# The first feed-forward's first product in seven block products, with two engines' orders written by hand

## The chip, the cores and the metric

The kernel runs on one core of a Trainium2 chip. The metric is the device time of one execution in microseconds, as the median of several runs. In the text PE is TensorE (matmul), PEld its weight loads, DVE is VectorE, ACT is ScalarE, POOL is GpSimd, and SP is the engine that only issues DMAs here. A letter q behind an engine's name means its instruction queue.

## The reference, cut to what matters

64 graphs of 256 nodes and 256 features go through two layers. The first is a graph attention layer with a feed-forward block of 1024 hidden features, the second a transformer layer with attention that is masked by relation, and a feed-forward block of its own. All is float32.

```python
# layer 0, per graph
h = gat(x, adj, W1, a1); h = gat(h, adj, W2, a2)      # softmax over neighbours, twice
h = layernorm(x + h, g_ln1, b_ln1)
ff = relu(h @ w_ff1 + b_ff1) @ w_ff2 + b_ff2          # h: 256x256, w_ff1: 256x1024
x = layernorm(h + ff, g_ln2, b_ln2)
# layer 1, per graph, 8 heads of 32
attn = softmax(q @ k.T / sqrt(32)); out = sum_r (attn * (adj == r)) @ v_r
x = layernorm(x + out @ Wo + bo, g1, beta1)
out = layernorm(x + gelu(x @ W1 + b1) @ W2 + b2, g2, beta2)
```

The change concerns the product h @ w_ff1 of layer 0, which is called the first feed-forward's first product.

## The kernel before, in words

Two graphs form a group of 512 tokens, so there are 32 groups. After a prologue the function `turn` is called 32 times. Each turn works on three groups at once, at different depths: group y is in layer 1 (attention, norm, second feed-forward), group x = y+1 is in the feed-forward of layer 0, and group z = y+2 is in the two graph attentions. An older group, y-1, still waits for its last norm, its affine step and its store (`waiting`, `finish`).

Attention of a group is cut into four quads (two graphs, four heads each). `scores(n)` makes the score products of quad n (L993), its four exponentials on ACT (L999), the masked copies ea (DVE, L1001) and the sums over node blocks es (DVE, L1004). `sums(n)` makes the weighted sums po and the totals zo on PE (L1014, L1017), and after every second quad `divided` the shares (DVE, L1025 to L1030). PE needs ACT and DVE to be done with a quad before its sums. To fill that time, eight blocks of the first feed-forward's first product (`hidden`, L804 on PE, relu on ACT at L806) stand between the quads in three groups: two, three and three blocks.

The second feed-forward's first product is already made from seven products of half the size each way (`hidden_seven`, L838). Its weights are combined once, on POOL (`seven`). For each turn DVE makes four differences of the moving operand (tt, L821). Each of the seven products comes twice, for halves a and b of the hidden features, and each half holds two PSUM banks, `one` and `two`. ACT copies a bank out to h1 (`copied`, L847), DVE adds a bank to h1 (`added`, L850), and ACT applies the function at the end (`done`, L856, and L880 for a whole row). A bank is written again by the next of the seven products only when it has been read out, so PE waits for ACT or DVE there.

After attention, `out_` multiplies by wo (yop, L766), with `project(z)` (xpp, L712) and `first_rows(z)` (L721) between. `normed` makes a norm: statistics on DVE (L780, L781), the inverse root on POOL (L782, L783), nm on DVE (L784), four applications on ACT (L787). `normed_features` transposes the normed rows (yt, DVE L666) and moves the pieces to their places by DMAs (L685 on SP's and ACT's queues, L675 on SP's) and four copies on POOL (L683, L675). PE meanwhile makes the first feed-forward's second product (yfp, L897, 64 instructions). Then come the second feed-forward's seven products, with the graph attention's sums (hpp, L755) between, then its second product, also of seven (`hidden_out_seven`, L918 on PE; four differences eq and eaq on DVE at L910 to L913; each partial result added to y by DVE at L923), and the graph attention of group z (L733 to L745, ygp at L766).

What sets the order: PE and SP run in the order of the code (`tc.manual_schedule`). The orders of DVE, ACT and POOL are made by the framework's scheduler; `behind(...)` only keeps an instruction from being put before a marked one. The stretch between the quads had, at L1137 and following,

```python
        scores(0)
        v = values(y_, hT, range(T))
        scores(1)
        piece()
        sums(0)
        first_hidden(range(0, 2))
        scores(2)
        sums(1)
        first_hidden(range(2, 5))
        scores(3)
        piece()
        first_hidden(range(5, 8))
```

and after it `early(z)` (the transposes of x and of the adjacency of group z on DVE, L1041 and L658), `load_x`, `finish` of the older group, `load_rows`, `sums(2)`, `sums(3)`. `checked` (DVE, L704) tests that the adjacency holds only 0 and 1.

Of the kernel before, what the change touches and what calls it, by code (L numbers as in the profile page):

```python
# [16 lines left out]
P = 128  # L17
# [368 lines left out]
def narrow_path(  # L386
# [213 lines left out]

    w1s, w2s = [], []

    def folding():

        shifted(wf1, range(FB // 2), lb1, bf1, "bf1")
        yield
        shifted(wf1, range(FB // 2, FB), lb1, bf1, "bf1")
        scaled(wf1, lg1)
        yield
        for w, bias, name in ((wq, bq, "bq"), (wk, bk, "bk")):  # L610
            shifted(w, range(KB), lb2, bias, name)
            scaled(w, lg2)
        yield
        ps = bank("rbvp")
        for k in range(KB):
            nc.tensor.matmul(ps, lb2[:, k:k + 1].to_broadcast([P, P]), wv[:, k].rearrange("p r f -> p (r f)"),
                             start=(k == 0), stop=(k == KB - 1))
        nc.vector.tensor_tensor(rbv, rbv, ps, ALU.add)
        scaled(wv.rearrange("p c r f -> p c (r f)"), lg2)
        shifted(w1, range(FB // 2), lb3, b1, "b1")  # L620
        yield
        shifted(w1, range(FB // 2, FB), lb3, b1, "b1")
        scaled(w1, lg3)
        w1s.extend(seven(w1, "w1"))
        w2s.extend(seven_out(w2, "w2"))
        yield
# [79 lines left out]

    def projected(u, hT):
        xp = work.tile([P, T, WX], F32, tag="wh", name=f"xp{u}")
        for t in range(T):
            ps = bank(f"xpp{u}_{t}")  # L710
# [13 lines left out]

    def gat_softmax(u, l, wh, rows, c, w, aT):

# [15 lines left out]
        nc.vector.reciprocal(z, z)  # L742
        nc.gpsimd.tensor_add(lowg, lowg, z)
        for t in range(T):
            mark["scaled"] = nc.scalar.activation(wh[:, t, :w], wh[:, t, :w], AF.Copy, scale=z[:, t:t + 1])  # L745
        return s

# [23 lines left out]
    def normed(u, l, y, blocks=range(T)):  # L771

        n, t0 = f"{u}_{l}_{blocks[0]}", blocks[0]
        bt = slice(t0, t0 + len(blocks))
# [4 lines left out]
        for t in blocks:  # L779
            nc.vector.bn_stats(st[:, t, :], y[:, t, :])  # L780
            nc.vector.bn_aggr(mv[:, t, :], st[:, t, :])  # L781
        nc.gpsimd.tensor_scalar(rs[:, bt], mv[:, bt, 1], EPS, 0.0, op0=ALU.add, op1=ALU.add)  # L782
        nc.gpsimd.tensor_tensor(rs[:, bt], rs[:, bt], mhalf[:, bt], ALU.pow)  # L783
        nc.vector.scalar_tensor_tensor(nm[:, bt], mv[:, bt, 0], -1.0, rs[:, bt],  # L784
                                       op0=ALU.mult, op1=ALU.mult)
        for t in blocks:
            mark["normed"] = nc.scalar.activation(y[:, t, :], y[:, t, :], AF.Identity,  # L787
                                                  bias=nm[:, t:t + 1], scale=rs[:, t:t + 1])
        if l == 3:
            nc.gpsimd.tensor_add(high[:, bt], high[:, bt], mv[:, bt, 0])  # L790

# [4 lines left out]

    def hidden(u, l, hT, wi, bi, func, blocks, h1=None):

        if h1 is None:
            h1 = work.tile([P, FB, TN], F32, tag="h1", name=f"h1{u}_{l}", bufs=1)  # L800
        for f in blocks:
            ps = bank(f"h1p{u}_{l}_{f}")
            for k in range(KB):
                nc.tensor.matmul(ps, wi[:, k, f * P:(f + 1) * P], hT[k],  # L804
                                 start=(k == 0), stop=(k == KB - 1))
            nc.scalar.activation(h1[:, f, :], ps, func, bias=bi[:, f:f + 1])  # L806
        return h1

    def hidden_seven(u, l, hT, w, bi, func, h1):

        a11, a12, a22, s1, s2, s3, s4 = w
        tt = work.tile([P, HPB, NB * N], F32, tag="e", name=f"tt{u}_{l}").rearrange("p a n -> p (a n)")
        quarter = [[hT[k][:, b * NB:(b + 1) * NB] for b in range(G)] for k in range(KB)]
# [42 lines left out]

        for h in halves:
            two[h] = bank(f"h1b{u}_{l}_{h}")  # L860
            product(two[h], h, a12, quarter[1][0], True)
            copied(h, 0, 0, two[h])
            one[h] = bank(f"h1a{u}_{l}_{h}")
            product(one[h], h, a11, quarter[0][0], True)
            added(h, 0, 0)
        yield
        for h in halves:
            product(two[h], h, s1, moving(0), True)
            copied(h, 1, 1, two[h])
        mark["fifth"] = mark["copied"]  # L870
        for h in halves:
            product(two[h], h, s4, quarter[1][1], False)
            copied(h, 0, 1, two[h])
        yield
        for h in halves:
            product(one[h], h, s2, moving(1), False)
            added(h, 0, 1)
            for i in range(2):
                f = 2 * h + i
                nc.scalar.activation(h1[:, f, :], h1[:, f, :], func, bias=bi[:, f:f + 1])  # L880
        yield
        for h in halves:
            product(one[h], h, s3, moving(2), False)
            added(h, 1, 1)
            done(h, 1, 1)
        yield
        for h in halves:
            product(one[h], h, a22, moving(3), False)
            done(h, 1, 0, one[h])

# [93 lines left out]
    def weighted(u, b, m, q, k_, aT):  # L984
# [13 lines left out]
        for a in range(HPB):  # L998
            mark[f"exp{b * KB + m}"] = nc.scalar.activation(e[:, a, :], ps[a], AF.Exp, scale=isd)  # L999
        for a in range(0, HPB, 2):  # L1000
            nc.vector.tensor_tensor(ea[:, a:a + 2, :], e[:, a:a + 2, :],  # L1001
                                    ab[:, None, :].to_broadcast([P, 2, NB * N]), ALU.mult)
        es = work.tile([P, HPB, N], F32, tag="es", name=f"es{n}")
        mark[f"summed{b * KB + m}"] = nc.vector.tensor_add(es, e[:, :, 0:N], e[:, :, N:2 * N])  # L1004
# [32 lines left out]
    def early(z):  # L1037
# [4 lines left out]
        d["xT"] = [xT[:, k] for k in range(KB)]  # L1042
        d["aT"] = adjacency(z, d["aq"])

    def project(z):
        d = g[z]
        d["xp"] = projected(z, d["xT"])

# [3 lines left out]
    def first_softmax(z):  # L1052
        d = g[z]
        d["s"] = gat_softmax(z, 0, d["xp"], d["rows"], F + 3, WH, d["aT"])

    def first_scores(z):
        first_rows(z)
        first_softmax(z)

    def second_rows(z):  # L1060
        g[z]["rows"] = score_rows(z, 1, g[z]["hp"], F)

    def second_softmax(z):
        d = g[z]
        d["s"] = gat_softmax(z, 1, d["hp"], d["rows"], F + 1, F, d["aT"])

# [18 lines left out]
    def out_pieces(u, y, h1, last):  # L1085
# [9 lines left out]
        for n, _ in enumerate(hidden_out_seven(u, 1, y, h1, w2s, *s)):  # L1095
            if last and n in (4, 6):
                finish(u, y, n // 6, 1)
            yield

    def finish(u, y, b, n, first=(), then=()):  # L1100

        bt = slice(b * NB, (b + n) * NB)
        with behind(*first):
            normed(u, 3, y, range(b * NB, (b + n) * NB))
        with behind(*then):
            affine(y[:, bt, :], rg4, rb4)
        nc.sync.dma_start(out[G * u + b:G * u + b + n].rearrange("b (c p) f -> p (b c) f", p=P), y[:, bt, :])

# [4 lines left out]
    def turn(y_, x_, z):  # L1113
# [8 lines left out]
        def scores(n):  # L1122
            e[n] = weighted(y_, *quads[n], q, k_, Y["aT"])

        def sums(n):
            b, m = quads[n]
            if m == 0:
                acc[b] = [psum.tile([P, 512], F32, tag=t_, name=f"{t_}{y_}_{b}") for t_ in ("po", "zo")]
            applied(b, m, v, *e.pop(n), *acc[b])
            if m == KB - 1:  # L1130
                divided(y_, b, *acc[b], oT)

        def first_hidden(blocks):
            if X:
                X["h1"] = hidden(x_, 0, X["hT"], wf1, bf1, AF.Relu, blocks, X.get("h1"))
            else:
                piece()  # L1137

        scores(0)
        v = values(y_, hT, range(T))  # L1140
        scores(1)
        piece()
        sums(0)
        first_hidden(range(0, 2))
        scores(2)
        sums(1)
        first_hidden(range(2, 5))
        scores(3)
        piece()
        first_hidden(range(5, 8))  # L1150
        if Z:
            early(z)
        if z + 1 < NG:
            load_x(z + 1)
        if waiting:
            finish(*waiting.pop(), 0, G, ("summed1", "exp2"), ("divided0",))
        if z + 1 < NG:
            load_rows(z + 1)
        sums(2)
        sums(3)  # L1160

        y = Y["y"]

        def out_(b):
            add_blocks(y_, "yop", y, b, lambda t, k: oT[:, k, t * P:(t + 1) * P],
                       lambda b, k: wo[:, k, :], KB)
        out_(0)
        piece()
        if Z:
            project(z)  # L1170
        out_(1)
        if Z:
            first_rows(z)
        normed(y_, 2, y)
        if X:
# [13 lines left out]
        h1 = work.tile([P, FB, TN], F32, tag="h1", name=f"h1{y_}_1", bufs=1)  # L1189
        for n, _ in enumerate(hidden_seven(y_, 1, hT, w1s, b1, AF.Gelu, h1)):  # L1190
            if Z and n > 1:
                Z["hp"] = gat_first(z, Z["s"], Z["xp"], Z.get("hp"), range(2 * n - 4, 2 * n - 2))
        if X:
# [6 lines left out]
        if z + 1 < NG:  # L1200
            load_adjacency(z + 1)
        if Z:
            second_rows(z)
# [21 lines left out]
    with tc.manual_schedule(engines={mybir.EngineType.PE, mybir.EngineType.SP}):  # L1225
# [19 lines left out]
        load_adjacency(2)  # L1245
        h1 = hidden(0, 0, g[0]["hT"], wf1, bf1, AF.Relu, range(FB))
        hidden_out(0, 0, g[0]["y"], h1, wf2)
        normed(0, 1, g[0]["y"])
# [60 lines left out]
```

## Time and profile before

| | us |
|---|---|
| median of 3 runs | 3142.31 (3139.66 to 3147.47) |
| the profiled execution | 3152.31 |
| its span, first to last instruction | 3150.7 |
| PE busy in the span | 3100.9 |
| DVE busy | 2234.9 |
| ACT busy | 1513.4 |
| POOL busy | 532.2 |
| PE busy in L804 (992 instructions on hT, 32 on h1T) | 450.6 and 16.3 |
| PE busy in L838 (1792 instructions) | 439.5 |

The page of a profile has one line for each group of equal instructions: line, engine, operation, what it writes and reads, shape and count; then busy time and the mean duration in ns of one; then the idle time of the engine just before them, and what ended most of it. The timeline has for each row the start and the duration in us, engine, line, operation, and in brackets the idle time of the engine before it with the instruction that ended it. An arrow `<-` in a name stands between what is written and what is read. The ends of matmuls are modelled, so rows overlap by some 0.16 us. The granted TensorE clock was 0.990 on average over the span, and 1.00 in the turn that is read.

### The profile page before, as it was taken

Reading aid. Unit: us, or ns where it says so; the run is one execution under the profiler, and the core shown is the slowest. Engines: PE = TensorE matmul, PEld = TensorE weight load, DVE = VectorE, ACT = ScalarE, POOL = GpSimd, SP = SyncE. Lnnn points to the kernel's source line nnn. Section 1 sums busy time; section 2 is a strip of 40 time slices with the busy share of each in tenths; the row PEclk is TensorE's granted clock in tenths of the full one; section 3 lists DMA queues with packets and bytes.
Section 4 is the critical chain, followed back from the end, with each engine's and each line's share of the span. In section 5 each row is a group of like instructions: output and inputs, shape, how many; then the busy total and the mean of one; then the engine's idle time right before and its main releaser. Section 6 shows DMA issues by size and latency. Waiting matters only on the chain. (4 is left out here: it accounts for less than half of the span.)

```text
span 3150.7 us, 50482 instructions
## 1 busy us (share of the span) xinstructions
PE 3100.9 (98%) x19120; PEld 2200.3 (70%) x19120; DVE 2234.9 (71%) x4280; ACT 1513.4 (48%) x2954; POOL 532.2 (17%) x822
## 2 busy tenths in 40 slices
PE   7999999999999999999999999999999999999997
PEld 5577766677766777666777666777666777667766
DVE  3577777776777777777777777777777777777665
ACT  4355544545544544545545445545445455445442
POOL 2121111111111111111211211211111211111100
PEclk8999999999999999999999999999999999999998
DMA  4011111111111111111111111111111111111000
GB/s 146 19 30 33 41 31 38 42 29 32 39 35 38 36 31 36 36 38 38 29 36 38 33 41 38 29 33 41 31 39 42 29 31 39 34 38 29 16 13 15
DMA packets 428537, 113.39 MB, mean 36 GB/s; under 512 B 364760, under 2 KB 427648, under 8 KB 428288
## 3 DMA queue, kind: packets, MB, share of 16 engines
q1 hardware_dynamic: 417952, 102.66, 14.9%
q10 hardware_dynamic: 9280, 6.39, 0.8%
q8 instruction: 153, 2.51, 0.3%
q0 software_dynamic: 1056, 1.05, 0.1%
q14 instruction: 96, 0.79, 0.1%
HBM read 57.04 MB, written 16.78 MB: 23 GB/s over the span
## 5 line engine op out<-in xcount | busy, mean ns | idle before, releaser
L804 PE MATMUL h1p<-hT,wf 128*128 128x512 f32 x992 | 450.6, 602 | 0.0
L897 PE MATMUL yfp<-wf,h 128*128 128x256 f32 x2048 | 447.3, 379 | 0.0
L897 PEld LDWEIGHTS yfp<-wf,h 128*128 128x128 f32 x2048 | 386.8, 190 | 51.8 <-issue 0.5
L787 ACT ACTIVATE y<-y,nm,rs 128x256 f32<-128x256 f32 x512 | 273.1, 598 | 249.7 <-DVE nm L784 245.4
L999 ACT ACTIVATE e<-sp 128x512 f32<-128x512 f32 x512 | 264.4, 602 | 249.3 <-PE sp L993 238.1
L1001 DVE TENSOR_TENSOR ea<-e,aT 128x1024 f32<-128x1024 f32 x256 | 312.4, 1261 | 70.9 <-ACT e L999 67.1
L804 PEld LDWEIGHTS h1p<-hT,wf 128*128 128x128 f32 x992 | 180.8, 190 | 228.6 <-issue 190.7
L806 ACT ACTIVATE h<-h1p,cols 128x512 f32<-128x512 f32 x256 | 176.9, 691 | 243.2 <-PE h1p L804 243.2
L683 POOL COPY hT<-yt 32x256 f32<-32x256 f32 x248 | 240.7, 971 | 185.1 <-DVE yt L666 177.3
L666 DVE STREAM_TRANSPOSE yt<-y 128x256 f32<-128x256 f32 x368 | 162.5, 442 | 97.4 <-ACT y L787 88.8
L782 POOL TENSOR_SCALAR rs<-mv 128x4 f32<-128x4 f32 (+1 forms) x130 | 54.6, 420 | 1043.5 <-DVE mv L781 1027.0
L977 PE MATMUL vp<-wv,hT 128*128 128x512 f32 x480 | 214.0, 599 | 0.0
L780 DVE BATCH_NORM_STATS2 st<-y 128x6 f32<-128x256 f32 x512 | 195.4, 414 | 5.6
L850 DVE TENSOR_TENSOR h<-h1a,h 128x512 f32<-128x512 f32 x192 | 131.0, 682 | 64.2 <-PE h1a L838 59.8
L966 ACT ACTIVATE q<-qp,cols 128x512 f32<-128x512 f32 x64 | 43.5, 679 | 262.5 <-PE qp L964 262.5
L993 PEld LDWEIGHTS sp<-q,k 32*128 32x128 f32 x2048 | 93.2, 184 | 108.1 <-issue 72.8
L714 ACT COPY xp<-xpp 128x260 f32<-128x260 f32 x128 | 48.1, 376 | 247.0 <-PE xpp L712 247.0
L977 PEld LDWEIGHTS vp<-wv,hT 128*128 128x128 f32 x480 | 88.7, 190 | 110.4 <-issue 103.2
L795 DVE TENSOR_TENSOR y<-y,rb 128x1024 f32<-128x1024 f32 (+1 forms) x130 | 161.7, 1245 | 3.3
L794 DVE TENSOR_TENSOR y<-y,rg 128x1024 f32<-128x1024 f32 (+1 forms) x130 | 157.3, 1210 | 5.0 <-ACT y L787 2.3
L1004 DVE TENSOR_TENSOR es<-e 128x1024 f32<-128x1024 f32 x128 | 155.8, 1217 | 0.0
L923 DVE TENSOR_TENSOR y<-yf,y 128x256 f32<-128x256 f32 x224 | 93.4, 417 | 87.7 <-PE yf L918 87.6
(217 smaller groups left out, 5686.0 us busy)
## 6 DMA issues: line engine op xcount, KB each, us to landing
hT<-yt SPq DMA_DIRECT2D x918, 32.0 KB, 2.0
y<-in_x_dram SPq DMA_DIRECT2D x32, 512.0 KB, 5.0
xq<-in_x_dram SPq DMA_DIRECT2D x240, 64.0 KB, 2.2
aq<-in_adj_dram SPq DMA_DIRECT2D x240, 64.0 KB, 2.4
out_dram<-y SPq DMA_DIRECT2D x30, 512.0 KB, 2.9
hT<-yt ACTq DMA_DIRECT2D x186, 32.0 KB, 1.9
wf<-in_L_gnn_w_ff_dram SPq DMA_DIRECT2D x2, 1024.0 KB, 7.3
w<-in_L_gnn_W_dram SPq DMA_DIRECT2D x2, 1024.0 KB
```

The source lines that it names most:

```text
L666: mark["transposed"] = nc.vector.transpose(yt[:, :, :, t].rearrange("p q k r -> p k q r"), xn[:, t].rearrange("p (k q c) -> p k q c", k=KB ...
L683: nc.gpsimd.tensor_copy(to, at)
L780: nc.vector.bn_stats(st[:, t, :], y[:, t, :])
L787: mark["normed"] = nc.scalar.activation(y[:, t, :], y[:, t, :], AF.Identity, bias=nm[:, t:t + 1], scale=rs[:, t:t + 1])
L794: nc.vector.tensor_mul(y, y, g_[:, None, :].to_broadcast(list(y.shape)))
L795: nc.vector.tensor_add(y, y, b_[:, None, :].to_broadcast(list(y.shape)))
L804: nc.tensor.matmul(ps, wi[:, k, f * P:(f + 1) * P], hT[k], start=(k == 0), stop=(k == KB - 1))
L806: nc.scalar.activation(h1[:, f, :], ps, func, bias=bi[:, f:f + 1])
L897: nc.tensor.matmul(ps[:, i * F:(i + 1) * F], h1[:, k, t * P:(t + 1) * P], wo_[:, k, :], start=(k == 0), stop=(k == FB - 1))
L977: nc.tensor.matmul(ps, hT[k][:, t * P:(t + 1) * P], wvf[:, k, :], start=(k == 0), stop=(k == KB - 1))
L999: mark[f"exp{b * KB + m}"] = nc.scalar.activation(e[:, a, :], ps[a], AF.Exp, scale=isd)
L1001: nc.vector.tensor_tensor(ea[:, a:a + 2, :], e[:, a:a + 2, :], ab[:, None, :].to_broadcast([P, 2, NB * N]), ALU.mult)
```

## The change

The eight blocks of the first feed-forward's first product are replaced by the seven products, with weights `wf1s` that POOL combines in the prologue. `hidden` is gone; `hidden_seven` no longer yields in a fixed order, but gives back a function that runs named steps: 2, 1, 5, 3, 6, 7 and 4 are the products with their copy or addition, r and s apply the function to rows that are done, and a or b names the half. The differences use the buffer of yt.

Inside the stretch from the first quad's masks to `early_adjacency`, DVE and ACT too run in the order of the code. `weighted` is cut into exponentials, `masked` and `node_sums`, `divided` is called apart (`shares`), and `normed` is cut into `norm` (statistics and POOL) and `applied_norm` (nm and the four applications). The older group's `norm`, `applied_norm` and `stored` (affine and store) stand at three places; the store and `load_rows` come behind `load_adjacency`. `load_x` comes ahead of `early`, `early` keeps only the transpose of x, and the adjacency's transpose (`early_adjacency`) comes behind the norm of group y. `project(z)` is cut into two halves. The scaling of xp (`first_scaled`) is put behind the copies of the fifth product of the second feed-forward.

```diff
@@ folding (prologue)
         scaled(wf1, lg1)
+        wf1s.extend(seven(wf1, "wf1"))
@@ turn, between the quads
-        scores(0)
-        v = values(y_, hT, range(T))
-        scores(1)
-        piece()
-        sums(0)
-        first_hidden(range(0, 2))
-        scores(2)
-        sums(1)
-        first_hidden(range(2, 5))
-        scores(3)
-        piece()
-        first_hidden(range(5, 8))
-        if Z:
-            early(z)
-        if z + 1 < NG:
-            load_x(z + 1)
-        if waiting:
-            finish(*waiting.pop(), 0, G, ("summed1", "exp2"), ("divided0",))
-        if z + 1 < NG:
-            load_rows(z + 1)
-        sums(2)
-        sums(3)
+        scores(0)
+        if z + 1 < NG:
+            load_x(z + 1)
+        with tc.manual_schedule(engines={getattr(mybir.EngineType, n) for n in
+                                         ("PE", "SP", "DVE", "Activation")[:4 if X else 2]}):
+            masks(0)
+            totals(0)
+            v = values(y_, hT, range(T))
+            steps = first_hidden(x_) if X else None
+            scores(1)
+            if Z:
+                early(z)
+            masks(1)
+            totals(1)
+            piece()
+            sums(0)
+            first("2a 1a 5a", 1)
+            scores(2)
+            sums(1)
+            shares(0)
+            first("3a 6a", 1)
+            masks(2, (0,))
+            first("2b 1b")
+            masks(2, (2,))
+            first("5b 7a 3b ra 6b")
+            totals(2)
+            first("4a 7b")
+            scores(3)
+            first("sa rb sb", 2)
+            masks(3)
+            totals(3)
+            sums(2)
+            last = norm(waiting[0][0], 3, waiting[0][1]) if waiting else None
+            if Z:
+                project(z, range(0, T // 2))
+            first("4b")
+            sums(3)
+            shares(1)
+            out_(0)
+            piece()
+            if Z:
+                project(z, range(T // 2, T))
+            out_(1)
+            if Z:
+                first_rows(z)
+            if waiting:
+                applied_norm(waiting[0][1], *last)
+            normed(y_, 2, y)
+            if Z:
+                early_adjacency(z)
@@ turn, second feed-forward
+        second("2a 1a 2b 1b 5a 5b")
+        if Z:
+            with behind("copied"):
+                first_scaled(z)
+        second("3a 3b 6a ra 6b rb")
...
         if z + 1 < NG:
             load_adjacency(z + 1)
+        if waiting:
+            with behind("added"):
+                stored(*waiting.pop(), slice(0, T))
+        if z + 1 < NG:
+            load_rows(z + 1)
@@ after the prologue's first norm
-        h1 = hidden(0, 0, g[0]["hT"], wf1, bf1, AF.Relu, range(FB))
-        hidden_out(0, 0, g[0]["y"], h1, wf2)
+        first_hidden(0)("2a 1a 2b 1b 5a 5b 3a 3b 6a ra 6b rb 7a sa 7b sb 4a 4b")
+        hidden_out(0, 0, g[0]["y"], g[0]["h1"], wf2)
```

The new function that names the steps, cut to its products:

```python
        def step(name):
            n, h = name[0], "ab".index(name[1])
            if n == "2":
                two[h] = bank(f"h1b{u}_{l}_{h}")
                product(two[h], h, a12, quarter[1][0], True)
                copied(h, 0, 0, two[h])
            elif n == "1":
                one[h] = bank(f"h1a{u}_{l}_{h}")
                product(one[h], h, a11, quarter[0][0], True)
                added(h, 0, 0)
            elif n == "5":
                product(two[h], h, s1, moving(0), True)
                copied(h, 1, 1, two[h])
            elif n == "3":
                product(two[h], h, s4, quarter[1][1], False)
                copied(h, 0, 1, two[h])
            elif n == "6":
                product(one[h], h, s2, moving(1), False)
                added(h, 0, 1)
            elif n == "7":
                product(one[h], h, s3, moving(2), False)
                added(h, 1, 1)
...
```

In the second feed-forward the order of the products is the same as before; only its steps are called by name. PE's lines shift: L838 becomes L837, L804 is gone, L923 becomes L928.

## The prediction, made before the changed kernel was run

> **What bounds the kernel now.** I read the page, then the waits of TensorE (PE), then the timeline of one turn, engine by engine. The page:
>
> ```profile
> span 3150.7 us, 50482 instructions
> PE 3100.9 (98%) x19120; PEld 2200.3 (70%) x19120; DVE 2234.9 (71%) x4280; ACT 1513.4 (48%) x2954; POOL 532.2 (17%) x822
> ...
> L804 PE MATMUL h1p<-hT,wf 128*128 128x512 f32 x992 | 450.6, 602 | 0.0
> ```
>
> PE is busy 98% of the span, and no idle time stands before L804, the product that is changed. Busy alone proves little, so I looked at who makes PE wait and at the spacing of its starts:
>
> ```profile
> PE sp L993 <- ACT k L966: 5.1, 30, 0.2
> ```
>
> This is the only wait of PE that recurs every turn: 0.2 us. The turn that starts at 1543.14 us (PE's timeline; start, us, engine, line):
>
> ```profile
> 1543.14 3.60 PE L964 MATMUL qp<-hT,wq 128*128 128x512 f32 x8
> 1546.58 3.60 PE L964 MATMUL kp<-hT,wk 128*128 128x512 f32 x8
> ...
> 1590.42 1.89 PE L766 MATMUL yop<-wo,q 128*128 128x256 f32 x8
> 1592.14 0.60 PE L721 MATMUL rows<-ident,xp 128*128 128x128 f32 x4
> ...
> 1606.40 1.03 PE L838 MATMUL h1b<-hT,w 128*128 128x256 f32 x4
> 1607.26 1.03 PE L838 MATMUL h1a<-hT,w 128*128 128x256 f32 x4
> ...
> 1609.85 1.89 PE L838 MATMUL h1b<-tt,w1s 128*128 128x256 f32 x8
> 1611.58 1.97 PE L838 MATMUL h1b<-hT,w1s 128*128 128x256 f32 x8
> 1613.38 1.89 PE L838 MATMUL h1a<-tt,w1s 128*128 128x256 f32 x8
> ...
> 1638.44 3.60 PE L964 MATMUL qp<-hT,wq 128*128 128x512 f32 x8
> ```
>
> A turn takes 1638.44 - 1543.14 = 95.30 us. From start to start a 512-column instruction takes 3.44/8 = 0.429 us, and a 256-column one (1606.40 to 1609.85, 16 of them) 0.216; each f32 product is two instructions. The seven-product form already runs there without gaps, except at 1611.58: 1.80 us for eight, 0.08 over 8 x 0.216. There PE waited for ScalarE (ACT) to copy a bank out. So PE is the bound, and what the change does to it counts nearly one for one, if nothing else becomes late.
>
> **What the Trainium skill says.** "Perfetto Trace Analysis", Identifying the Most-Contended Engine: matmul busy share is no good measure; hence the spacing. "TensorE: Matmul & The Clock Gate", Back-to-back issue gap: N/2.4 + 2.5 ns; the trace has 216 and 429 ns, which is this formula at twice the columns (215.8, 429.2). Same page, Architectural detail: PE pulls weight loads ahead, ACT and VectorE (DVE) are strict FIFOs. The 0.08 us agrees with the first; the second is why their order decides below. "ScalarE: Activation LUTs", Table sets: relu is in every set, so relu from another place loads no table; the trace agrees (loads at L880 and L737, none at L806).
>
> **The change, part by part.** t counts us from a turn's start. Orders are those of the built program, durations those of this turn.
>
> *1. Fewer columns.* 32 x 0.4294 = 13.74 us become 56 x 0.2158 = 12.09: -1.65. The row-tiled and column-tiled attention products pay about 0.1 at each change to or from the full array. The order scores(3), sums(2), xpp, 4b, sums(3) has nine changes where eight were: +0.14.
>
> *2. Handovers inside the seven products.* A product's end to ACT's start is 0.20, the copy 0.58, its end to PE's next effective start 0.16: 0.94, and one product between covers 0.864. So 0.08 of wait, as at 1611.58. It stands so at 5a (1a covers), 5b (1b) and 3b (7a): 0.24. Before 7b the sum on DVE lies between (0.20 + 0.69 + 0.16 = 1.05, covered by 4a): 0.19. The other steps have two or more products between. Sum +0.43; floor 0, ceiling 1.0 if DVE's queue is behind. I walked it: the four differences (1.7 us) follow the last v at t 16.05, the masks of quad 1 end at 21.1 and its sums at 22.3, needed at 22.7 and 24.4. ACT gains six copies and eight short activations for eight long ones, some 3 us in a stretch where it is half idle: nothing. First half of the turn: -1.65 + 0.14 + 0.43 = -1.08, so yop_1 ends at t 47.92 (before 49.00).
>
> *3. The way from yop_1 to the second feed-forward's input.* Before:
>
> ```profile
> 1595.58 0.16 DVE L784 SCALAR_TENSOR_TENSOR nm<-mv,rs 128x4 f32<-128x4 f32 x1 [1.54 <-POOL rs L783]
> 1596.41 1.92 DVE L666 STREAM_TRANSPOSE yt<-y 128x256 f32<-128x256 f32 x4 [0.67 <-ACT y L787]
> 1598.48 3.91 SPq L685 DMA_DIRECT2D hT<-yt  x6
> ```
>
> yt is done at t 55.19; the last move is issued at t 58.7, lands 1.9 later (60.6), and PE reads it at 63.26: 2.7 us of slack. After: add at 48.12; then nm of the delayed norm, and all four statistics alternate with their aggregates (0.53 a pair instead of two pairs ahead): 51.05. GpSimd and nm_2 as before (1.7): 52.75. ACT's four norms of the older output stand ahead, but end at 51.0. Then DVE runs the adjacency transpose (1.24) ahead of yt, and the check of the adjacency (1.23) between the third and fourth yt: yt ends at 56.55. Moves as before (3.4 + 1.9): 61.9, plus 0.16 for PE: 62.05. PE has finished yfp at 62.18. Slack 0.1: I take a stall of 0.1; floor 0, and each us later costs a us.
>
> *4. The output stage.* DVE now has the older output's affine (2.5 us; before, at L795 in the first half) between the last added and the first difference, where it idled:
>
> ```profile
> 1621.33 1.23 DVE L910 TENSOR_TENSOR eq<-h 128x1024 f32<-128x1024 f32 x1 [1.87 <-ACT h L856]
> ...
> 1626.27 0.42 DVE L923 TENSOR_TENSOR y<-yf,y 128x256 f32<-128x256 f32 x1
> ```
>
> ACT scales xp after the copies of 5b, ahead of those of 3a and 3b, and puts three of the four norms of the other group behind gelu. Counted from that product's start S: last gelu S+12.9, last short activation S+17.0, norms to S+18.4; DVE's three yt wait for them (S+18.9), two differences follow (S+21.2), then the first sum L923, S+21.5. PE's fourth product reads its bank after that sum: effective S+21.65, and PE is there at S+21.45: stall 0.2. Before the slack was 1.0. Floor 0, ceiling 1.0 (each op there may be 0.05 longer, over some 20). Later waits hold: hp is scaled at S+26.5, wanted at S+27.0; the next hT leaves 4 us.
>
> *5. SP's queue.* The store and the load of rows move behind the adjacency loads; SP is free again at about t 3 of the next turn, when the load has waited for the store (2.9 us, as L441 does now), and the next yt asks at t 6.5: nothing. If late, hT_0's slack goes first. The load of x moves ahead, but still waits for DVE's transpose: nothing. wf1s costs GpSimd 4 x 1.27 us at about 42 us of the span, inside its 8.3 us of idle: nothing.
>
> *Sum.* A full turn: -1.08 + 0.1 + 0.2 = -0.78; 29 such turns: -22.6. Turns 0 (no older output) and 30 (no next group): -1.1 each. First group's product ahead of the turns: -1.65 + 0.43 = -1.2. Together -26.0. The profiled execution took 3152.3 (span 3150.7 and 1.6 around it), so it would take 3126.3. The median of the runs is 3142.3, 10 less; the same saving there gives 3116.3.
>
> **The rivals.**
>
> *A, as summed*: 3116.3, own range 3101 to 3132 (a turn gains 1.3 to 0.25). For it: PE has no other wait. Chance 0.48.
>
> *B, no stall in parts 2 to 4*: -1.51 x 31 - 1.65 = -48.5, so 3093.8. Against it: the 0.08 at 1611.58. Chance 0.12.
>
> *C, the gain is given back in the output stage*: the stall before the fourth product, or before ygp, is 0.9 instead of 0.2. A turn gains 0.08, the sum is 2.3 + 3.4: 3136.6. For it: ACT and DVE are in series there, with 20 steps. Chance 0.20.
>
> *D, slower: the second feed-forward waits for its input.* Place: the first L838 product after yfp. Mechanism: DVE's two adjacency instructions and the serial statistics hold yt back, and PE has nothing else to do. It is decided at hT's landing: at t 62.9 instead of 61.9 the turn's gain of 0.88 is gone (the gain without the 0.1 allowed for this stall). At 63.5, 1.6 late, a turn costs 0.62 more, 29 turns 18, less 3.4: 3156.9. For it: a slack of 2.7 falls to 0.1. Against it: the walk has no link in it that the trace doesn't show. Chance 0.17.
>
> *E, the change does not do what it says* (the products still wait for one another and nothing is saved, 3142): the built program has the 56 instructions in each turn; 0.03.
>
> **How the numbers follow.** A measurement of this kernel tells 0.3% (9.4 us) from no change. Faster is A and B with a little of C: 0.62. Same is most of C, A's edge and E: 0.20. Slower is D and C's tail: 0.18. The range leaves out half of B's side below 3096 and D's far part above 3150.
>
> **What would show it.** In the profile after: a turn of about 94.5 us; L837 with 56 instructions more per turn at 0.216; waits of L837 on ACT of 0.08 three times a turn and on DVE of 0.2 once; yt of the second feed-forward done 8.6 us after yop_1 ends (before 6.2); no wait of PE for hT beyond 0.2; a wait of 0.2 before the fourth output product for L928. I am wrong if hT makes PE wait over 0.5 us a turn, if L928 or hp does so for over 0.7, or if the sums of attention wait for es or ea.

## The result and the profile after

The changed kernel takes 3128.64 us in the median of four runs (3128.14 to 3133.72), the kernel before 3142.15 in four (3139.66 to 3147.47): a ratio of 0.9958, 95% interval 0.9941 to 0.9976. That is 13.5 us less, where 26.0 were forecast. The interval leaves out no change at all, so the kernel is faster, and the median lies inside rival A's own range (3101 to 3132 us); but half of the saving did not come. The same kernel on another chip (run e9), in five rounds, gave 3132.24 against 3145.52, again 0.9958 (0.9944 to 0.9971).

The page of the kernel after (span; busy time and instructions of each engine):

```profile
span 3126.4 us, 52820 instructions
PE 3067.8 (98%) x19888; PEld 2327.7 (74%) x19888; DVE 2383.2 (76%) x4600; ACT 1626.6 (52%) x3274; POOL 602.5 (19%) x826
```

PE is still the bound at 98%. It has 768 instructions more: 56 shorter ones in each of 31 turns and in the first group's product, where 32 stood. DVE went from 2234.9 to 2383.2 us. The waits of PE in the kernel after (us in total, times, longest):

```profile
PE yf L923 <- DVE y L928: 7.0, 30, 1.5
...
PE sp L998 <- ACT k L971: 5.0, 30, 0.2
...
PE h1b L837 <- DVE s L738: 0.6, 1, 0.6
PE h1b L837 <- DMA hT<-yt: 0.3, 1, 0.3
```

The second line stood in the kernel before too. The first is new and comes every turn, but for its longest time (1.5), which stood in the kernel before too: the output stage. The last two are two single turns in which the input of the second feed-forward came late. The view gives the first line 0.2 us a time, and the spacing of the starts shows more, so here is one turn of PE's timeline (start, us, engine, line), the one that answers to the turn shown of before:

```profile
1534.00 3.60 PE L969 MATMUL qp<-hT,wq 128*128 128x512 f32 x8
...
1566.12 2.15 PE L837 MATMUL h1a<-tt,wf 128*128 128x256 f32 x8
1568.20 1.15 PE L998 MATMUL sp<-q,k 32*128 32x256 f32 x16
...
1581.99 0.60 PE L723 MATMUL rows<-ident,xp 128*128 128x128 f32 x4
...
1596.24 1.03 PE L837 MATMUL h1b<-hT,w 128*128 128x256 f32 x4
...
1615.90 1.95 PE L923 MATMUL yf<-w,h 128*128 128x128 f32 x16
1618.04 2.05 PE L923 MATMUL yf<-w2t,eq 128*128 128x128 f32 x16 [0.19 <-DVE y L928]
1619.93 3.74 PE L923 MATMUL yf<-w,eaq 128*128 128x128 f32 x32
```

The end of the turn, which is the start of the next qp, stands at 1628.74: a turn of 94.74 us. Four distances carry the reading. From 1534.00 to 1581.99, where the second product with wo (yop_1) ends and rows begins, the first half took 47.99 us (before 49.00). The eight rows (single matmul instructions) of 4a and 7b from 1566.12 to 1568.20 took 2.08 us for 1.73: there lie the 0.26 of the handover before 7b and 0.09 of the change to the row-tiled scores (sp), which use 32 of PE's 128 rows each. The second feed-forward starts at 1596.24, right behind yfp: no wait. From 1615.90 to 1618.04 the third output product took 2.14 us where sixteen rows at 0.1115 take 1.78: 0.36, and the first row of the fourth takes 0.10 more, so 0.45 of wait in all.

| in us from the turn's start | before | forecast | after |
|---|---|---|---|
| yop_1 ends | 49.00 | 47.92 | 47.99 |
| yt of the second feed-forward done | 55.19 | 56.55 | 56.41 |
| first product of the second feed-forward | 63.26 | 62.28 | 62.24 |
| from there to the turn's end | 32.04 | 32.24 | 32.50 |
| turn | 95.30 | 94.52 | 94.74 |

By the starts of qp the kernel after gained 14.85 us in the 29 full turns, 0.47 in turn 0, 0.02 in turn 30 and about 0.3 in the first group's product.

### The profile page after: what moved, and what is told of

The parts are those of the page before. It is cut to its first block, busy times and chain, and to the rows that moved or that the text cites. A ratio compares the mean times of both kernels' runs of the same rounds, so it can differ in the third digit from the quotient of the medians.

```text
span 3126.4 us, 52820 instructions
## 1 busy us (share of the span) xinstructions
PE 3067.8 (98%) x19888; PEld 2327.7 (74%) x19888; DVE 2383.2 (76%) x4600; ACT 1626.6 (52%) x3274; POOL 602.5 (19%) x826
## 3 DMA queue, kind: packets, MB, share of 16 engines
q0 software_dynamic: 1056, 1.05, 0.1%
## 5 line engine op out<-in xcount | busy, mean ns | idle before, releaser
L846 ACT COPY h<-h1b 128x512 f32<-128x512 f32 x384 | 221.2, 584 | 333.9 <-PE h1b L837 331.5
L849 DVE TENSOR_TENSOR h<-h1a,h 128x512 f32<-128x512 f32 x384 | 263.9, 687 | 130.8 <-PE h1a L837 93.7
L684 POOL COPY hT<-yt 32x256 f32<-32x256 f32 x248 | 240.3, 969 | 215.9 <-DVE yt L667 187.9
L676 POOL COPY hT<-yt 32x256 f32<-32x256 f32 x120 | 111.0, 925 | 392.3 <-DVE yt L667 388.6
L880 ACT ACTIVATE h<-h,cols 128x512 f32<-128x512 f32 x256 | 167.5, 718 | 1.5 <-DVE h L849 1.1
L667 DVE STREAM_TRANSPOSE yt<-y 128x256 f32<-128x256 f32 x368 | 148.1, 428 | 25.0 <-ACT y L800 20.0
L998 PE MATMUL sp<-q,k 32*128 32x256 f32 x2048 | 147.3, 400 | 6.8 <-ACT k L971 5.0
L1024 PE MATMUL po<-e,v 128*32 128x256 f32 x2048 | 137.0, 385 | 0.0
```

The lines of the kernel that those rows point to most:

```text
L684: nc.gpsimd.tensor_copy(to, at)
L846: mark["copied"] = nc.scalar.copy(out(h, o, b), pair(ps))
L849: mark["added"] = nc.vector.tensor_tensor(out(h, o, b), pair(one[h]), out(h, o, b), ALU.add)
L998: nc.tensor.matmul(ps[a][:, j * N:(j + 1) * N], k_[hp, m, j0:j0 + P], q[hp, m, b * N:(b + 1) * N], start=True, stop=True)
```

## The experiments

The period of a full turn is read from PE's timeline and repeats to 0.05 us in most turns, much finer than the medians, so it is what most of these runs are for. It is 94.75 us in the kernel after on its first chip and 94.80 on the chip of e9, where e5, e7 and e8 ran too. The table gives the usual turn. Each ratio is to runs of the kernel before on the same chip, whose medians were 3142.15 (first measurement), 3143.70 (e1 to e4) and 3145.52 us (e5, e7, e8 and e9); e6 ran on a third chip, where the kernel before took 3141.28 in one run.

| kernel | turn, us | device time, us (95% interval of the ratio to before) |
|---|---|---|
| before | 95.30 | 3142.15 |
| after | 94.75 | 3128.64 (0.9941 to 0.9976) |
| e1, older output stored late | 94.41 | 3120.96 (0.9914 to 0.9947) |
| e2, two products between | 94.25 | 3113.62 (0.9892 to 0.9925) |
| e3, one transpose more | 95.30 | 3144.33, one run |
| e4, eight blocks in the new orders | 95.95 to 96.24 | 3173.85, one run |
| e5, orders by the scheduler | 97.23 | 3207.31, one run |
| e6, xp scaled early | 95.62 | 3156.82, one run |
| e7, one transpose more, second try | 95.68 to 95.97 | 3169.48, one run |
| e8, e1 and e2 and one edit more | 93.94 | 3107.70 (0.9864 to 0.9894) |
| e9, after once more | 94.80 | 3132.24 (0.9944 to 0.9971) |

### e1: the older output's affine behind the output products

```diff
-        if waiting:
-            with behind("added"):
-                stored(*waiting.pop(), slice(0, T))
-        if z + 1 < NG:
-            load_rows(z + 1)
...
+        # after the loop over the output products
+        with behind("summed", "quarters"):
+            stored(*waiting.pop(), slice(0, T))
+        if z + 1 < NG:
+            load_rows(z + 1)
```

> The older output's affine (two VectorE instructions, 2.5 us) and its store stand after the output stage's products instead of ahead of the four differences. Theory: TensorE's wait before the fourth output product (0.45 us a turn) comes from VectorE's queue, of which this affine is the head. Without it the first difference still waits for ScalarE's last short activation of 7b (some 0.3 us earlier than now), so the wait falls by 0.35 to about 0.1, as it stands in turn 0, which has no older output. A turn takes 94.40 us instead of 94.75, the whole some 10 us less than the changed kernel. Rival 1: the wait comes from the three norms that ScalarE runs late, and from the transposes that wait for them; then the affine's place changes nothing, a turn stays at 94.75. Rival 2: the affine in its new place holds up the transposes of the next turn's input, and TensorE waits there; a turn takes 95 or more.

Measured: 94.41. The timeline of PE at the same place:

```profile
1611.28 1.95 PE L923 MATMUL yf<-w,h 128*128 128x128 f32 x16
1613.08 2.05 PE L923 MATMUL yf<-w2t,eq 128*128 128x128 f32 x16
```

1.80 us from the third product to the fourth, where it was 2.14, and no wait is named. The first row of the fourth product still takes 0.10 more, which is what is left of the wait. So moving the affine took away 0.34 of the 0.45. By DVE's timeline the first difference starts 0.31 us earlier. The scheduler also put the third difference ahead of the transposes, which costs some 0.2 again, and the last difference takes 1.18 us instead of 1.42. Neither rival holds: the norms alone would have left the wait as it was, and the next turn's input is not late.

### e2: two products between a bank's fill and its next use

```diff
-            first("2a 1a 5a", 1)
+            first("2a 1a", 1)
             scores(2)
             sums(1)
             shares(0)
-            first("3a 6a", 1)
+            first("5a 2b 1b", 1)
             masks(2, (0,))
-            first("2b 1b")
+            first("3a 5b 6a")
             masks(2, (2,))
-            first("5b 7a 3b ra 6b")
+            first("pb 3b")          # p: product 6 alone, q: its sum
             totals(2)
-            first("4a 7b")
+            first("qb 7a")
             scores(3)
-            first("sa rb sb", 2)
-            masks(3)
-            totals(3)
             sums(2)
+            masks(3)
+            first("ra rb sa 7b 4a sb")
+            totals(3)
```

> The fourteen products of the first feed-forward in another order, so that every product stands at least three places after the one whose bank it waits for, except that 7b to 4b has other work between; the product of scores(3) and sums(2) move up by two products. Theory: the waits of TensorE inside the fourteen products (0.08 three times and 0.26 before 7b, 0.50 in all) are the time of a handover (product, copy or sum, next product: 0.94 to 1.05 us) less one product (0.864), and two products between cover it: a turn takes 94.25 us instead of 94.75. Rival: the waits come from the queues of VectorE and ScalarE, which are full there; then they go elsewhere and a turn takes 94.6 to 95.2.

Measured: 94.25. PE's timeline, the second stretch of products:

```profile
1360.99 1.03 PE L837 MATMUL h1b<-hT,wf 128*128 128x256 f32 x4
...
1367.04 1.03 PE L837 MATMUL h1a<-tt,wf 128*128 128x256 f32 x4
```

From 1360.99 to 1367.04 there are 28 rows in 6.05 us, 0.216 each: not one of them waits, and none waits in the two other stretches of this turn. The kernel after lost 0.08 three times and 0.26 once. The turn is shorter by the 0.50 that these waits made, so two products between cover a handover, and the waits did not go elsewhere.

### e3 and e7: a longer way to the second feed-forward's input

e3 runs the transpose of the adjacency twice:

```diff
-        nc.vector.transpose(aT.rearrange("p t n -> p (t n)"), aq.rearrange("p t n -> p (t n)"))
+        for _ in range(2):
+            nc.vector.transpose(aT.rearrange("p t n -> p (t n)"), aq.rearrange("p t n -> p (t n)"))
```

> VectorE runs the transpose of the next adjacency twice, 1.24 us more ahead of the transposes of y that feed the second feed-forward; nothing else changes. Theory: the way from yop_1 to that input has 0.1 to 0.2 us of slack in the changed kernel, so TensorE waits 1.05 to 1.15 us for hT and a turn takes 95.8 to 95.9 us, 29 turns some 31 us more. Rival: the trace shows no wait of TensorE for hT because there is room of a microsecond or more, and a turn stays at 94.75 to 94.85.

Measured: 95.30, between the two forecasts, and PE does not wait for hT: the first product of the second feed-forward stands at 62.25 from the turn's start. The edit had missed its aim. The scheduler put the check of the adjacency behind the transposes of y, not between them, so yt was not later. The half microsecond arose further on: DVE's other work came later, and 6b of the second feed-forward waited 0.58 us for the sum of 1b. So e3 says nothing on the slack. In e7 the second transpose stands ahead of the statistics, and the check stays between the transposes of y:

```diff
-            normed(y_, 2, y)
             if Z:
                 early_adjacency(z)
+            normed(y_, 2, y)
+            if Z:
+                nc.vector.transpose(Z["aT"].rearrange("p t n -> p (t n)"), Z["aq"].rearrange("p t n -> p (t n)"))
```

> The first lengthening of the way to the second feed-forward's input missed its aim: the scheduler took the check of the adjacency out from between the transposes, which made up for it. Here one more transpose of the adjacency (1.24 us) stands ahead of the statistics, and the other transpose and the check stay where they are. Theory: slack of 0.1 to 0.2 us, so TensorE waits 1.05 to 1.15 us for hT and a turn takes 95.8 to 95.9, up to 96.4 if VectorE's fuller queue costs the half microsecond in the second feed-forward that it cost in that first attempt. Rival: there is room of over a microsecond; the wait for hT stays below 0.2.

Measured: 95.68 to 95.97 in all turns but two, in a pattern of three or four turns. PE's timeline:

```profile
1423.78 1.10 PE L837 MATMUL h1b<-hT,w 128*128 128x256 f32 x4 [0.90 <-DVE s L738]
```

yfp starts at 1408.90, so its 64 rows at 0.216 are over at 1422.72; PE starts at 1423.78 and its first row takes 0.08 more, so it waited 1.14 us. The view names DVE's L738, which only happens to end there; the tile that PE reads is hT, moved by DMA. The longer way brings yt 1.13 us later (57.55 from the turn's start; 56.42 in e9 on the same chip), since the second transpose overlaps its neighbours by some 0.1. Without turns 6 and 9 it cost 0.87 to 1.19 a turn, so the slack is between nothing and 0.26.

### e4: the old eight blocks in the new orders

The eight 512-column blocks (relu on ACT behind each) stand where the pairs of products stood. They read the weights as the kernel after leaves them, one quarter replaced by a difference, so the values differ from the reference's; the work is that of the kernel before.

```diff
+    # block f: two products of 512 columns, one activation
+    eight = {"1a": (0,), "5a": (1,), "3a": (2,), "1b": (3,), "7a": (4,), "6b": (5,), "7b": (6,), "4b": (7,)}
...
+        if x_ > 0:
+            return hidden(x_, 0, X["hT"], wf1, bf1, AF.Relu, X["h1"])
```

> The changed kernel with its hand-written orders, but with the old eight 512-column blocks in the turns (seven products only in the one ahead of the turns). The blocks stand where the pairs of products stood. Theory: the seven products save 1.65 us of columns and pay 0.50 in waits, the orders themselves save nothing; a turn takes 94.75 + 1.15 = 95.90 us, which is 0.6 over the kernel before (95.30), the price of the hand-written orders and the moved steps (0.14 of changes between row-tiled and full products, 0.45 before the fourth output product). Rival: the orders are a gain of their own, and a turn takes 95.3 or less.

Measured: 95.95 in the quietest turns, some 96.2 in most others (up to 0.3 of wait at the first product of the second feed-forward), up to 97.2 in a few. The seven products alone are worth 1.15 us up to yop_1, which ends at 49.14 from the turn's start here and at 47.99 in the kernel after: the 1.65 of columns less the 0.50 of waits. The rewritten order around them costs 0.65 and more against the kernel before: 0.14 up to yop_1, as part 1 forecast, 0.51 to 0.54 from the second feed-forward on, and the wait for its input on top. The order is the price, not a gain of its own.

### e5: the same order of products, DVE and ACT left to the scheduler

```diff
-        with tc.manual_schedule(engines={getattr(mybir.EngineType, n) for n in
-                                         ("PE", "SP", "DVE", "Activation")[:4 if X else 2]}):
+        with tc.manual_schedule(engines={getattr(mybir.EngineType, n) for n in
+                                         ("PE", "SP")}):
```

> The changed kernel with the first half of a turn written down by hand for TensorE and the DMA queue only; the scheduler orders VectorE and ScalarE. It then puts the masks and sums of the third scores (3.6 us) and the shares ahead of the sum of 6a on VectorE, and the relu of a half ahead of the copy of 5b on ScalarE. Theory: 7a waits 1.8 us for that sum and 3b some 0.9 for that copy, so a turn takes about 97.3 us (96.5 to 98) instead of 94.75, and the seven products without the hand-written orders are slower than the kernel before (95.30). Rival: the orders of the two engines matter little, since TensorE's order is the same; a turn stays within 0.3 of 94.75.

Measured: 97.23. DVE's timeline and PE's:

```profile
1401.70 2.36 DVE L1009 TENSOR_TENSOR ea<-e,aT 128x1024 f32<-128x1024 f32 x2 [0.94 <-ACT e L1004]
...
1406.78 0.65 DVE L849 TENSOR_TENSOR h<-h1a,h 128x512 f32<-128x512 f32 x1
```

```profile
1407.49 1.13 PE L837 MATMUL h1a<-tt,wf 128*128 128x256 f32 x4
1409.33 1.13 PE L837 MATMUL h1b<-hT,wf1s 128*128 128x256 f32 x4 [0.70 <-ACT h L846]
```

The masks and sums of the third scores and the shares stand ahead of the sum of 6a, and 3b starts 1.84 us behind 7a instead of 0.864. The sum was as expected, its parts were not: 7a lost only 0.35 to the late sum and 3b 0.87 to the copy of 5b, and by the spacing of the starts 0.11 were lost in kp, 0.32 in the values and 0.81 in the second scores, which was not foreseen. That the whole came out right is luck. What holds is that with this order of PE and the scheduler's orders of DVE and ACT the kernel is 1.9 us a turn slower than the kernel before; another order of PE under the scheduler was not tried.

### e6: xp scaled at its old place

```diff
             with behind("transposed", "placed"):
                 first_softmax(z)
+                first_scaled(z)
...
-        if Z:
-            with behind("copied"):
-                first_scaled(z)
```

> The changed kernel with the scaling of xp on ScalarE back at its old place, ahead of the copies of the second feed-forward's products; the three norms of the other group then stand between the copies as in the kernel before, and VectorE's three transposes leave the queue ahead of the fourth output product's sum. Theory: ScalarE takes its instructions strictly in order, so the copies wait for the scaling, which waits for VectorE's z, ready 2.4 us after the first product of the second feed-forward; the third pair of products (5a) then waits 1.4 us for the copy of 2a, while the wait before the fourth output product (0.45) goes to nothing: a turn takes 95.7 us. Rival: the place of the scaling is indifferent, and the turn only gains the 0.45: 94.3 us.

Measured: 95.62. ACT's timeline and PE's:

```profile
1421.14 1.71 ACT L750 ACTIVATE xp<-xp,z 128x258 f32<-128x258 f32 x4 [1.51 <-DVE z L744]
1422.76 1.04 ACT L846 COPY h<-h1b 128x512 f32<-128x512 f32 x2
```

```profile
1423.37 1.99 PE L837 MATMUL h1b<-tt,w1s 128*128 128x256 f32 x8 [1.05 <-ACT h L846]
```

The copy of 2a, whose product had ended at about 1419.6, ran at 1422.76: ACT sat behind the scaling, and the scaling behind z. This is the strict order that the forecast took from the Trainium skill ("TensorE: Matmul & The Clock Gate", Architectural detail), and the trace agrees: here it cost 1.32 us (5a starts 2.08 behind the start of 1b instead of 0.864, and its first row takes 0.10 more). With the transposes out of DVE's queue the wait before the fourth output product was nothing: the third and fourth product stand 1.79 apart. So the affine (e1) and the three late transposes (e6) both lie in that chain, and either one's removal nearly empties the wait.

### e8 and e9: the edits together, and the changed kernel again

e8 joins e1 and e2 and moves, in turn 30 alone, the older output's statistics behind the shares:

```diff
-            last = norm(waiting[0][0], 3, waiting[0][1]) if waiting else None
+            last = norm(waiting[0][0], 3, waiting[0][1]) if waiting and Z else None
...
             shares(1)
+            if waiting and not Z:
+                last = norm(waiting[0][0], 3, waiting[0][1])
             out_(0)
```

> Three edits together: the order with two products between, the older output's affine and store after the output products, and in turn 30 the older output's statistics behind the shares of the second half (they stood ahead of them, and TensorE waited 1.9 us for the shares where nothing else was left to do). Theory: the gains add up, a turn takes 94.75 - 0.50 - 0.35 = 93.90 us and turn 30 some 0.8 less than with the order alone; the median is 3102 to 3104 us. Rival: with TensorE faster the affine in its new place delays the next turn's input or the fourth output product waits longer; a turn takes 94.1 or more and the median is above 3107.

> The changed kernel once more, unaltered, timed in five rounds against the kernel before on the same chip as the three edits. From its steady turns the change saves 29 x 0.55 = 16.0 us, from turn 0 and the first product 0.5 to 1.5 more, nothing in turn 30: some 17 us, so a median some 17 us below that of the kernel before. If only the 13.5 of the first measurement is found again, part of the saving in the turns is lost at the ends.

Measured: e8 93.94 a turn against 94.80 of e9 on the same chip, so the 0.86 of e1 and e2 add up; 3107.70 us against 3132.24, and 1.2% below the kernel before. The median expected, 3102 to 3104, was too low: that chip is 0.05 us a turn slower, a few of e8's turns take up to 1.1 us longer, and the third edit gave nothing (turn 30 takes 75.51 us, and 75.38 in e2 without it): e2's order had already brought the masks forward, so that the statistics were over before the shares were due. e9 found the first measurement's saving again, 13.3 us, and not the 17 that I had expected from the turns.

## Why the prediction was half right

*Columns and handovers (parts 1 and 2): right, 0.07 off.* The first half gained 1.01 a turn of 1.08. The three waits of 0.08 were there to the hundredth. Only the one before 7b was 0.26 instead of 0.19: 0.15 on the last row of 4a and 0.10 on its own first. e2 showed that a second product between takes all four away, e4 that the seven products bring what the columns less the handovers are. Rivals B (no stalls at all) and E (nothing saved) fell with them.

*The way to the second feed-forward's input (part 3): right to 0.14.* DVE's timeline after:

```profile
1586.71 1.24 DVE L659 STREAM_TRANSPOSE aT<-aq 128x1024 int32<-128x1024 int32 x1
1587.87 1.06 DVE L667 STREAM_TRANSPOSE yt<-y 128x256 f32<-128x256 f32 x3
...
1589.96 0.45 DVE L667 STREAM_TRANSPOSE yt<-y 128x256 f32<-128x256 f32 x1
```

yt is done at 56.41; the stall of 0.1 did not come in 27 of the 29 turns. e7 measured the slack at between nothing and 0.26. Rival D's mechanism was therefore real and a hair away. It did decide in two turns. Turn 9 has yt and the issue of the last move at the same places as any other (56.40 and 59.86), and still

```profile
1027.69 1.10 PE L837 MATMUL h1b<-hT,w 128*128 128x256 f32 x4 [0.60 <-DVE s L738]
```

starts at 63.01 instead of 62.24. Turns 6 and 9 lost 0.53 and 0.84; what ran beside their moves is told in the last section.

*The output stage (part 4): the term that was mis-sized.* The forecast put the end of the first sum of the output products (L928) at S+21.5, and so a stall of 0.2. DVE's timeline after (S, the start of the second feed-forward's first product, is 1596.24), and POOL's:

```profile
1614.09 1.12 DVE L667 STREAM_TRANSPOSE yt<-y 128x256 f32<-128x256 f32 x3
1615.13 1.18 DVE L917 TENSOR_TENSOR eaq<-h,eq 128x1024 f32<-128x1024 f32 x1
1616.23 1.42 DVE L918 TENSOR_TENSOR eaq<-h 128x1024 f32<-128x1024 f32 x1
1617.57 0.74 DVE L928 TENSOR_TENSOR y<-yf,y 128x256 f32<-128x256 f32 x2
```

```profile
1615.34 3.84 POOL L676 COPY hT<-yt 32x256 f32<-32x256 f32 x4 [12.93 <-DVE yt L667]
```

The third transpose ends at S+18.97 (forecast 18.9), and until there the walk holds. Then the two differences end at S+21.41 instead of 21.2: they take 2.44 us instead of 2.3, since the last one takes 1.42 in all 29 full turns, where it took 1.22 in the kernel before, from which I had the figure. The sum ends at S+21.74 and PE follows 0.16 later, at S+21.90, while it could have gone on at S+21.45: 0.45 instead of 0.2. So mechanism and place were as forecast, and 0.25 a turn, 7.3 us in 29 turns, were too little: 0.14 from the two differences, 0.07 from the steps ahead of them, the rest from the sum. That is the largest part of what is missing; it lies within the ceiling that I gave (1.0), a third of the way from rival A's 0.2 to rival C's 0.9. e1 and e6 show that DVE's queue is what the wait hangs on. Why the last difference takes 0.2 longer was not tried by an edit of its own, but the traces of all runs narrow it down. It starts while one of POOL's copies of hT still has 0.3 us to run; in the kernel before and in e6 none runs beside it and it takes 1.22, and in e1 a copy only starts during it and it takes 1.18. The full turns of the eleven traces hold 7652 DVE operations of this kind (TENSOR_TENSOR, 128x1024 f32). All 6088 that start with no copy of hT running on POOL take 1.18 to 1.23 us. In the other 1564 the time goes with what is left of the copy: 1.20 to 1.22 with 0.1 us or less, 1.24 to 1.30 with 0.2, 1.35 to 1.42 with 0.3. By this reading the late transposes cost twice: they stand ahead of the last two differences, and POOL's copies, which wait for them, run into the last one.

*Turns 0 and 30 and the first product: taken at a full turn's 1.1, wrongly.* In turn 30 nothing was gained. The older output's statistics stand by hand ahead of the shares:

```profile
2995.30 0.42 DVE L787 BATCH_NORM_STATS2 st<-y 128x6 f32<-128x256 f32 x1
...
2997.43 0.68 DVE L1035 STREAM_TRANSPOSE rz<-zo 128x512 f32<-128x512 f32 x1
```

The shares start 2.13 us behind the first of them. In a full turn xpp covers that; in turn 30 there is no next group, and PE waited:

```profile
3000.02 1.97 PE L770 MATMUL yop<-wo,q 128*128 128x256 f32 x8 [1.76 <-DVE q L1040]
```

The second yop started 2.76 us behind the first in the kernel before and 3.75 in the kernel after: 0.99 lost, against the 1.0 that the products had gained. The first group's product gained 0.3 of 1.2, since PE now waits 1.06 longer for what DVE makes ahead of it; turn 0 gained 0.47 of 1.1.

*The sum.* Forecast 22.6 + 2.2 + 1.2 = 26.0. Measured in the traces 14.85 + 0.49 + 0.3 = 15.6. Of the 10.4 missing, 7.3 are the output stage, 2.0 the first half, 1.4 the two turns with late input, 2.6 the ends; 2.9 came back since the 0.1 for hT was not needed. The medians say 13.5 and 13.3, with intervals of 7.5 to 18.5 and 9.1 to 17.6 us; the last 2 us between trace and median were not told apart. The conversion from the profiled execution of before (3152.3) to the medians held: the profiles differ by 24.2, and some 5 of the 8.6 that exceed 15.6 are PE rows at half rate, as told below.

## What to carry to other kernels

Where a forecast leaves a stall of some tenths at the end of a long chain, its size is worth as much care as the operations that are saved: here 0.25 us a turn made 7 us of 26, more than half of it from one duration that was measured where no copy ran beside it on POOL. When a product waits for its bank, count the products between fill and next use: a handover took 0.94 to 1.05 us, one product 0.864, and a second product between was worth 0.50 us a turn. First and last turns need a walk of their own, because the work that hides a moved step is missing there.

## What the runs showed of the hardware that was not expected

After the same wait for the same copy, the same eight products ran at half rate in one kernel and at full rate in the other. PE's timeline of before, then of after, at the start of the last turn:

```profile
3049.58 6.76 PE L964 MATMUL qp<-h2T,wq 128*128 128x512 f32 x8 [2.68 <-ACT h2T L652]
```

```profile
3031.96 3.70 PE L969 MATMUL qp<-h2T,wq 128*128 128x512 f32 x8 [2.67 <-ACT h2T L653]
```

The rows stand 0.853 us apart in the first and 0.429 in the second. The Trainium skill, "TensorE: Matmul & The Clock Gate", Part 1, calls the number of products at the half rate variable from run to run. The eleven traces agree in part. After waits of 2.67 to 2.71 us these eight products ran at half rate throughout in two traces, at full rate in five, and changed rate on the way in four. But most of the traces are of different kernels, and the kernel after, profiled twice, showed full rate both times; so whether one kernel varies from run to run is not shown here. Over the first 120 and the last 100 us the rows at half rate cost some 15 us in the profile of before and 10 in that of after, so a difference of single profiled executions is no measure of a change of this size.

After every wait of PE that is read here the first row takes 0.08 to 0.10 us more than the rhythm. The weight loads (PEld) show what is different. In the rhythm a row's weights start to load one row ahead, 0.21 us before it. For the product that waited at 1611.58 in the kernel before they started at 1611.55, and for the fourth output product of the kernel after at 1618.04, together with the row itself. So the load did not run ahead of the wait.

The two turns of late input are the same two, 6 and 9, in e9 on another chip (0.89 and 0.64 us there). In turn 6 two of the twelve issues of moves, one on ACT's queue and one on SP's, took 1.38 and 1.10 us where 0.60 is usual, so that ACT's six take 4.89 us instead of 3.73:

```profile
736.27 4.89 ACTq L686 DMA_DIRECT2D hT<-yt  x6
```

In turn 9 all issues are in place, but the last packet of the moves ends at 61.93 from the turn's start, where it ends at 61.42 in turn 13.

In both turns of both executions a packet of the DMA queue that the profile calls instruction runs among the moves. It moves 16 KB in 1.11 us in turn 6 and 8 KB in 0.58 in turn 9 (1.45 and 0.50 in e9). Eight traces have a usual wait for hT below 0.35 us and a small slack: after, e1 to e4, e6, e8 and e9. In eleven of their turns a 16 KB packet stands among the moves, and in all eleven the input was late, by 0.31 to 1.34 us; e4's four longest turns are among them. In turn 20 of the kernel before and in three turns of e5 such a packet ran there too, but PE did not wait for hT, since the slack is over 2 us there. Packets of 8 KB mostly cost nothing. No run was made to test this, so the packet is a likely cause and not a shown one.
